# Scores of a cross-attention kernel: from four row tiles of TensorE to eight row-and-column tiles

## The chip, the cores and the metric

The kernel runs on one core of a Trainium2 chip. The metric is the device time of one execution in microseconds, from the runs of the kernel; beside it stands one execution that the hardware profiler recorded, with its trace.

## What is computed

Sixteen batches. `x` is 16 x 100 x 640, the context is 16 x 722 x 384, of which the last 4 tokens (`ca`) are treated apart and 718 are keys and values. There are 8 heads of 80 columns, all in f32. Cut to what matters:

```python
query = x @ Wq                       # 100 x 640
keyt, valt = enc @ Wk, enc @ Wv      # 718 x 640
hs = mha(query, keyt, valt)          # the scores of this change are in here
ca_q1 = einsum('btc,th->bch', ca, Wq_ca)[:, indices]
ca_hs1 = mha(ca_q1, x, x)
ca_hs2 = mha(ca_hs1 @ Wq, ca @ Wk_ca, ca @ Wv_ca)
out = (hs + ca_hs2) @ Wout + b_out + x

def mha(q, k, v):                    # per head, d = 80
    scores = q @ k.T * d ** -0.5     # 100 x 718
    return softmax(scores) @ v
```

## The kernel before, in words

One long program without loops on the device; Python writes out all instructions, batch after batch, and from the first batch on each engine executes them in the order in which they are written (`manual_schedule`). TensorE, VectorE (DVE), ScalarE (ACT), GpSimd (POOL) and SyncE (SP) wait for each other by semaphores.

The 718 keys of a batch lie in three thirds `u` of 240 (they overlap by a key), each in two halves `j` of `KN` = 120 keys: six blocks `KC`. The transposed keys are in `kT`, [128, 5, 3, 240]: the head dimension of 80 is cut into 64 + 16, and spread so that chunks `c` = 0 to 3 hold, in each of the four groups of 32 partitions (row groups, `r`), 32 rows of one head; chunk 4 holds the remaining 16 rows of two heads in each row group. The queries lie in the same way in `qp` (chunks 0 to 3, 100 columns per product) and `qz` (chunk 4, where two heads' queries stand side by side with zeros, 200 columns).

`scores(b, g, tiles)` is called three times in a batch, for `g` = 0, 1, 2, each for two of the six blocks (`a` = 0, 1). For every block and chunk it issues one product in each row group (L612): 32 rows, 120 key columns as weights, 100 or 200 query columns streamed, into the PSUM bank `s_ps[r]` of that row group. That is 2 x 5 x 4 = 40 products for each `g`, 120 in a batch, 1920 in all. A product in f32 shows in the trace as two weight loads (PEld) and two matmuls (PE). The banks of `g` = 0 and 2 come as two pairs from the pool `ps2`, the four of `g` = 1 from `psk` and `ps1`. ScalarE copies them to the tile `st` (L629 for the pairs, L623 for the single banks); VectorE folds `st` into a running maximum `most` (L1246, L1234).

The order of a batch on TensorE around the scores: the products of probabilities and values of the batch before (`a_ps`, L1419: pairs of column tiles, 64 and 36 query rows), the scores (L612), then `z_ps` (L788, `softmax2`: four column tiles of 32, 32, 32 and 4 rows, 33 columns streamed), then `y_ps` (L736), and then the long stretch in which this batch's values (`v_ps...`, L432) and the next batch's keys (`k_ps...`, L463, and `kT_ps`, L557) are made, with the output projection (`o_ps`, L1013) or the next queries (`q_ps`, L533) in some batches. Meanwhile VectorE and ScalarE turn the maximum, subtract it (L1222) and take the exponentials (L1230), and GpSimd makes sums for the keys and values (L498) and the second attention (L761, L768, L855, L862).

## Time and profile before

| | us |
|---|---|
| median of 3 runs | 931.06 |
| lowest and highest of them | 929.72, 931.26 |
| profiled execution: span from the first to the last instruction | 929.5 |
| TensorE matmuls busy | 922.4 (99%) |
| TensorE weight loads busy | 787.6 (85%) |
| VectorE busy | 693.2 (75%) |
| GpSimd busy | 678.2 (73%) |
| ScalarE busy | 433.9 (47%) |

For the profiled execution no other time than its span is given; it lies within the runs' lowest 0.3 us. PE are matmuls and PEld weight loads, which go beside each other. Matmuls are pipelined and their recorded ends are modelled, so times from start to start say more than durations. "issue" as the releaser of idle time means that the engine waited for nothing that the profile shows. Queues of the kind "instruction" bring the engines' own code from memory.

### The profile page before, as it was taken

The numbers are of one execution on the slowest core, as the hardware profiler recorded it, in microseconds if no ns is written. First come the engines' busy times: TensorE is split into PE (matmuls) and PEld (weight loads), VectorE is DVE, ScalarE is ACT, GpSimd is POOL, SyncE is SP. The second block draws the span as 40 slices with busy tenths as digits, with TensorE's granted clock in tenths as the row PEclk, the third lists the DMA queues.
The fourth block names the chain that finished last, engine by engine and source line by source line (L and its number), as shares of the span: only waits on it lengthen the run. The fifth ranks groups of instructions, "written<-read, shape, count | busy, mean of one in ns | idle before, by whom it ended". The sixth has DMA issues, their size and how long they took to land.

```text
span 929.5 us, 25894 instructions
## 1 busy us (share of the span) xinstructions
PE 922.4 (99%) x11130; PEld 787.6 (85%) x11130; DVE 693.2 (75%) x1085; ACT 433.9 (47%) x836; POOL 678.2 (73%) x646
## 2 busy tenths in 40 slices
PE   9999999999999999999999999999999999999998
PEld 6998989797897979888798788988879888797966
DVE  3859895989739896685967869579873888838884
ACT  2234543736337363652726436264641737427341
POOL 5757998788938877496884968758895578956724
PEclk9999999999999999999999999999999999999999
DMA  8722022040300304031030400205030050310201
GB/s 262 264 85 77 25 66 76 7 149 2 117 17 23 105 13 120 2 103 53 28 105 3 120 36 30 75 2 154 2 103 30 2 154 2 102 45 2 82 19 41
DMA packets 49673, 62.82 MB, mean 68 GB/s; under 512 B 14072, under 2 KB 38200, under 8 KB 49560
## 3 DMA queue, kind: packets, MB, share of 16 engines
q1 hardware_dynamic: 45512, 51.49, 18.3%
q0 software_dynamic: 3024, 8.53, 3.0%
q8 instruction: 87, 1.43, 0.6%
q10 hardware_dynamic: 1024, 1.15, 0.4%
q14 instruction: 26, 0.21, 0.1%
HBM read 55.59 MB, written 5.57 MB: 66 GB/s over the span
## 4 chain that ended last, share of the span: by engine, by line
PE 97%; DVE 2%; DMA 0%; issue 0%; ACT 0%; POOL 0%; ACTq 0%; DVEq 0%
PE s_ps L612 12%; PE a_ps L1419 12%; PE v_psA L432 11%; PE v_psB L432 9%; PE kT_ps L557 8%; PE k_psA L463 7%; PE q_ps L533 7%; PE k_psB L463 6%; PE o_ps L1013 5%; PE v_psC L432 3%; PE k_psC L463 3%; PE v_psD L432 2%; PE v_psE L432 2%; PE y_ps L736 2%; PE v_ps L373 1%; PE k_psE L463 1%
## 5 line engine op out<-in xcount | busy, mean ns | idle before, releaser
L761 POOL TENSOR_TENSOR e<-ca,g 100x800 f32<-100x800 f32 x64 | 99.4, 1564 | 126.8 <-DVE most L1234 99.7
L498 POOL TENSOR_TENSOR enc<-enc 128x240 f32<-128x240 f32 x135 | 106.7, 800 | 19.7 <-DMA enc<-in_enct 12.7
L1222 DVE TENSOR_TENSOR st<-st,over 120x1600 f32<-120x1600 f32 x48 | 117.0, 2439 | 0.0
L1419 PEld LDWEIGHTS a_ps<-vs,st 120*36 120x36 f32 (+3 forms) x3072 | 109.3, 125 | 5.9 <-issue 5.8
L1419 PE MATMUL a_ps<-vs,st 120*36 120x81 f32 (+3 forms) x3072 | 112.2, 233 | 0.9 <-issue 0.9
L432 PE MATMUL v_psA<-wv_sb,enc 128*120 128x320 f32 x352 | 109.8, 434 | 0.0
L862 POOL TENSOR_TENSOR hs<-hs,hs 100x640 f32<-100x640 f32 x48 | 100.5, 2095 | 3.8
L612 PE MATMUL s_ps<-qp,kT 32*120 32x100 f32 x3072 | 97.5, 263 | 0.0
L855 POOL TENSOR_TENSOR hs<-vb,p 100x640 f32<-100x640 f32 x64 | 89.6, 1411 | 9.5 <-issue 4.7
L612 PEld LDWEIGHTS s_ps<-qp,kT 32*120 32x120 f32 x3072 | 94.7, 179 | 1.7 <-issue 0.2
L629 ACT COPY st<-s_ps 120x800 f32<-120x800 f32 x64 | 49.7, 828 | 98.1 <-PE s_ps L612 98.1
L768 POOL TENSOR_TENSOR e<-e,e 100x800 f32<-100x800 f32 x48 | 92.0, 1917 | 3.8
L432 PE MATMUL v_psB<-wv_sb,enc 128*120 128x320 f32 x296 | 91.8, 433 | 0.0
L1230 ACT ACTIVATE st<-st 120x1600 f32<-120x1600 f32 x48 | 73.9, 1539 | 32.3 <-DVE st L1222 32.1
L463 PE MATMUL k_psA<-enc,wk_sb 128*128 128x240 f32 x360 | 87.7, 366 | 0.0
L1234 DVE TENSOR_TENSOR most<-most,st 120x800 f32<-120x800 f32 x64 | 69.0, 1078 | 21.9 <-ACT st L623 20.8
L463 PEld LDWEIGHTS k_psA<-enc,wk_sb 128*128 128x128 f32 x360 | 68.3, 190 | 16.7
L432 PEld LDWEIGHTS v_psA<-wv_sb,enc 128*120 128x120 f32 x352 | 63.2, 183 | 22.6 <-DVE vs L403 0.5
L463 PE MATMUL k_psB<-enc,wk_sb 128*128 128x240 f32 x300 | 73.1, 366 | 0.1
L432 PEld LDWEIGHTS v_psB<-wv_sb,enc 128*120 128x120 f32 x296 | 54.1, 183 | 21.9 <-DVE vs L403 0.4
L928 ACT COPY hsT<-turned_hs 32x160 f32<-32x160 f32 (+7 forms) x244 | 67.7, 278 | 3.0
L533 PE MATMUL q_ps<-xT,wq_sb 128*128 128x200 f32 x400 | 69.1, 333 | 0.0
(168 smaller groups left out, 1802.9 us busy)
## 6 DMA issues: line engine op xcount, KB each, us to landing
vb<-va_d POOLq DMA_DIRECT2D x32, 250.0 KB, 3.5
vb<-va_d SPq DMA_DIRECT2D x32, 250.0 KB
enc<-in_enct SPq DMA_DIRECT2D x30, 240.0 KB
enc<-in_enct SPq DMA_DIRECT2D x15, 360.0 KB
xT<-in_xt SPq DMA_DIRECT2D x8, 500.0 KB
rest<-in_enct SPq DMA_DIRECT2D x31, 120.0 KB
xn<-in_x SPq DMA_DIRECT2D x11, 320.0 KB
out<-xn SPq DMA_DIRECT2D x11, 320.0 KB
```

The source lines that it names most:

```text
L432: nc.tensor.matmul(at[0][j][:KN, : H // 2], a_form(self.enc, f)[:, j * KN : (j + 1) * KN], wv_there.get(f, wv_sb[:, W_AT[f]]), start=first ...
L463: nc.tensor.matmul(at[:, i * KT : (i + 1) * KT], wk_sb[:, W_AT[f], i], a_form(self.enc, f), start=(first and i == 0), stop=last, skip_grou ...
L498: nc.gpsimd.tensor_tensor(out, left, right, op)
L533: nc.tensor.matmul(q_ps[:, : 2 * S].rearrange("p (j s) -> p j s", j=2), wq_sb[:, c, n * P : (n + 1) * P], xT[:, :, c, :], start=(c == 0), ...
L557: nc.tensor.matmul(bank[:, i * KT : (i + 1) * KT], weights[c], a_raw(enc, u, c), start=(i == 0 and c == 0), stop=(c == CC - 1), skip_group ...
L612: nc.tensor.matmul(s_ps[r][:n, 256 * a + lo : 256 * a + hi], kT[rows, c, u, j * KN : (j + 1) * KN], rhs, start=(a == 0 and c == 0), stop=( ...
L761: first = nc.gpsimd.tensor_tensor(to, self.ca[:, t, :].unsqueeze(1).to_broadcast([S, NH, S]), g[:, :, t].unsqueeze(2).to_broadcast([S, NH, ...
L768: nc.gpsimd.tensor_tensor(e, e, to, ALU.add)
L855: first = nc.gpsimd.tensor_tensor(to, self.vb[t][:S].rearrange("p (h d) -> p h d", h=NH), p2[:, :, t].unsqueeze(2).to_broadcast([S, NH, D] ...
L862: nc.gpsimd.tensor_tensor(sums, sums, to, ALU.add)
L1222: return nc.vector.tensor_tensor(st[i], st[i], top.over[:KN].unsqueeze(1).to_broadcast([KN, 2, ROWS]), ALU.subtract,)
L1419: nc.tensor.matmul(a_v[lo:hi, h % 4], st[i // 2][: KEYS[i], i % 2, h * S + lo : h * S + hi], block(i, h // 4)[: KEYS[i], h % 4], start=(i ...
```

## The change

In `scores`, each product of a row group is written as two: keys 0 to 63 of the block go to the PSUM partitions 0 to 63, keys 64 to 119 to the partitions 64 to 119 of the same bank. With the four row groups, TensorE is then used as eight tiles of 32 rows by 64 columns. The streamed queries, the banks, the copies and the order of everything else remain. 1920 products become 3840, so the scores' weight loads and matmuls go from 3840 each to 7680 each. All lines below L612 in the file move down by one.

```diff
                         rhs, lo, hi = qz[rows, 0, b % 2], 0, 2 * S
-                    nc.tensor.matmul(
-                        s_ps[r][:n, 256 * a + lo : 256 * a + hi],
-                        kT[rows, c, u, j * KN : (j + 1) * KN],
-                        rhs,
-                        start=(a == 0 and c == 0),
-                        stop=(c == HC - 1),
-                        skip_group_check=True,
-                    )
+                    for k0, k1 in ((0, 64), (64, n)):
+                        nc.tensor.matmul(
+                            s_ps[r][k0:k1, 256 * a + lo : 256 * a + hi],
+                            kT[rows, c, u, j * KN + k0 : j * KN + k1],
+                            rhs,
+                            start=(a == 0 and c == 0),
+                            stop=(c == HC - 1),
+                            skip_group_check=True,
+                        )
```

## The prediction

> **What bounds the kernel now.** I read the page first, then the groups of instructions with their shapes kept apart, then one batch in the timeline, then the stages around the change, and last the few places where TensorE stood still without a wait. The page:

> ```profile
> span 929.5 us, 25894 instructions
> PE 922.4 (99%) x11130; PEld 787.6 (85%) x11130; DVE 693.2 (75%) x1085; ACT 433.9 (47%) x836; POOL 678.2 (73%) x646
> ...
> q8 instruction: 87, 1.43, 0.6%
> ...
> PE 97%; DVE 2%; DMA 0%; issue 0%; ACT 0%; POOL 0%; ACTq 0%; DVEq 0%
> PE s_ps L612 12%; PE a_ps L1419 12%; PE v_psA L432 11%; PE v_psB L432 9%; PE kT_ps L557 8%; PE k_psA L463 7%; PE q_ps L533 7%; PE k_psB L463 6%; PE o_ps L1013 5%; PE v_psC L432 3%; PE k_psC L463 3%; PE v_psD L432 2%; PE v_psE L432 2%; PE y_ps L736 2%; PE v_ps L373 1%; PE k_psE L463 1%
> ```

> TensorE is the bound from end to end, and the scores are 12% of that chain. So each microsecond that the scores win or lose shows in the span, as long as TensorE stays the last. One line matters later: 11130 loads and 11130 matmuls go through TensorE, and queue q8 brings 87 packets of instructions. 22260 / 87 is 256 instructions to a packet of 16 KB: this is TensorE's own code, fetched while it runs.

> The scores' line (durations minimum / median / maximum), and the loads of other widths:

> ```profile
> L612 PEld LDWEIGHTS s_ps<-qp,kT x3072: 174/180/180, 60.0 to 885.6; 32*120 32x120 f32 x192
> L612 PE MATMUL s_ps<-qp,kT x3072: 244/263/342, 60.0 to 885.7; 32*120 32x100 f32 x192
> L612 PE MATMUL s_ps<-qz,kT x768: 327/338/413, 60.9 to 886.0; 32*120 32x200 f32 x192
> ```
> ```profile
> L1419 PEld LDWEIGHTS a_ps<-vs,st 120*64 120x64 f32 x1024 | 84.5, 136 | 5.9 <-issue 5.8
> ...
> L463 PEld LDWEIGHTS k_psA<-enc,wk_sb 128*128 128x128 f32 x360 | 68.3, 190 | 16.7
> ...
> L788 PEld LDWEIGHTS z_ps<-y_sb,e 100*4 100x4 f32 x256 | 9.1, 84 | 0.0
> ```

> Per batch there are 120 products in the scores, and (3072 + 768) / 16 = 240 matmuls and 240 loads: each f32 product is two loads and two matmuls. A hundred more columns stream in 327 - 244 = 83 ns. Loads of 128 and of 4 columns differ by 106 ns, 0.855 ns a column: a load of 120 columns occupies its row group for 103 ns, one of 64 for 55. So today a 100-column product is bound by its load (103), not by its stream (83). One batch in the timeline:

> ```profile
> 431.77 1.10 PE L612 MATMUL s_ps<-qp,kT 32*120 32x100 f32 x32
> 432.69 0.54 PE L612 MATMUL s_ps<-qz,kT 32*120 32x200 f32 x8
> 433.05 1.00 PE L612 MATMUL s_ps<-qp,kT 32*120 32x100 f32 x32
> ...
> 438.58 0.54 PE L612 MATMUL s_ps<-qz,kT 32*120 32x200 f32 x8
> 439.05 0.75 PE L788 MATMUL z_ps<-y_sb,e 100*32 100x33 f32 x64
> ```

> From 432.69 to 438.58 lie five blocks of keys, 1.178 us each. Per row group that is 8 steps of 103 ns and 2 of 167 (200 columns, stream-bound): 1.158, so the reading holds.

> The same batch by stages: attention times values (a_ps), scores, z_ps, and all that follows up to the next a_ps (columns: window, its length, then busy time and count of TensorE's matmuls, its loads, VectorE, ScalarE and GpSimd, the granted clock, DMA share, GB/s).

> ```profile
> 424.85:431.77 6.92, 6.92 (x193) 6.82 (x193) 4.53 (x7) 0.87 (x1) 6.61 (x9) 1.00 0.27 99
> 431.77:439.05 7.28, 7.28 (x243) 7.04 (x241) 4.00 (x6) 3.23 (x6) 3.17 (x4) 1.00 0.01 2
> 439.05:439.72 0.67, 0.67 (x68) 0.63 (x64) 0.64 (x2) 0.52 (x1) 0.00 (x0) 1.00 0.11 24
> 439.72:481.22 41.50, 41.50 (x208) 35.12 (x199) 35.68 (x55) 23.05 (x49) 32.55 (x29) 1.00 0.24 74
> ```

> **The change, first part: what the array gains.** Each product of 120 key columns becomes two, of 64 and 56, in the two column tiles of its row group. The longer load now takes 55 ns and hides behind the 83 ns stream. That column tiles run side by side shows in a_ps, which already pairs 64 with 36 columns: 193 matmuls in 6.92 us are 72 ns a pair, against 81 x 0.83 = 67 for one stream; two after another would be 134. The extra is 5 ns. So a step becomes 83 + 5 = 88 and a 200-column step 167 + 5 = 172: 8 x 88 + 2 x 172 = 1.048 us instead of 1.178. Six blocks in 16 batches: 96 x 0.130 = 12.5 us less, if the instructions are there in time.

> Nothing else in the order moves; ScalarE's copies (L629, L623) and VectorE's maxima (L1246, L1234) stay behind the scores. Were the scores faster, the cover would be this: copies of group 0 must free their banks before group 2 starts.

> ```profile
> 434.49 1.55 ACT L629 COPY st<-s_ps 120x800 f32<-120x800 f32 x2 [5.22 <-PE s_ps L612]
> 436.83 1.68 ACT L623 COPY st<-s_ps 120x400 f32<-120x400 f32 x4 [0.79 <-PE s_ps L612]
> 439.20 1.55 ACT L629 COPY st<-s_ps 120x800 f32<-120x800 f32 x2 [0.69 <-PE s_ps L612]
> ```

> A group would last 2.10 us and the longest set of copies 1.68, so ScalarE keeps up; at worst some 0.1 us a batch returns, 2 us in all.

> **Second part: what the change adds.** The scores' instructions double: per batch 480 more loads and matmuls, 7680 in all, 30 more packets of code. Does code arrive fast enough? Now it does, barely: 480 instructions in 7.28 us are 3.9 us for 256. Three places show what happens when it does not. TensorE stops with nothing to wait for, in the middle of a_ps and in the middle of z_ps:

> ```profile
> 760.82 2.22 PE L1419 MATMUL a_ps<-vs,st 120*36 120x81 f32 x58
> 763.91 0.79 PE L1419 MATMUL a_ps<-vs,st 120*64 120x81 f32 x17 [0.87 <-issue]
> ```
> ```profile
> 381.10 0.57 PEld L788 LDWEIGHTS z_ps<-y_sb,e 100*32 100x32 f32 x57 [0.24 <-issue]
> 381.94 0.15 PEld L788 LDWEIGHTS z_ps<-y_sb,e 100*32 100x32 f32 x7 [0.26 <-issue]
> ```

> Between the two restarts TensorE ran this many instructions:

> ```profile
> 381.93:763.90 381.97, 381.11 (x4442) 325.33 (x4442) 291.62 (x460) 190.12 (x374) 286.31 (x265) 1.00 0.21 61
> ```

> 8884, and its semaphore instructions, which are not counted there; 35 packets would be 8960. The stops lie at the edge of a packet. And the code packets stand right before them. The DMA view, in the windows 379.0 to 380.6, then 761.2 to 762.5, then 765.0 to 766.0 (764.0 to 765.0 holds none):

> ```profile
> q8 instruction: 1, 0.02, 5.3%
> ```
> ```profile
> q8 instruction: 1, 0.02, 5.6%
> ```
> ```profile
> q8 instruction: 1, 0.02, 5.8%
> ```

> [...]

> **The sum.** Scores and z_ps (another 128 instructions) come to 1088 a batch, 4.25 packets. About one is in hand when the scores start: half of the one entered, on average, and the next one in half of the batches or nearly there. That one runs at its own pace, 1.68 us; the other 3.25 take 3.6 each, 11.7. Together 13.4 us against 7.28 + 0.67 = 7.95 now: 5.45 more a batch, 87 us in 16. What follows draws 208 matmuls and 199 loads in 41.5 us, 26 us for 256, so it loses nothing and gives nothing back; the other engines have more time than now. The profiled span of 929.5 becomes 1017; the median of the runs, 931.06, lies 1.5 above it and becomes 1018.

> Bounds: with 1.09 + 0.93 + 1.34 = 3.36 for a packet it is +74, with 1.16 + 1.36 + 1.54 = 4.06 it is +111; with half a packet more or less in hand 15 us less or more. As both ends hardly meet, together 995 to 1050. Below nothing only if the fetch hides, which is a rival.

> **Rivals.** *The fetch hides* (faster). If more than one packet is held ahead or a packet comes in under 1.93 us (3.25 times that plus 1.68 is today's 7.95), the array's gain is left: 931 - 12.5, 918.5, up to 920.5 with the copies' 2 us. For it: steps and loads fit the trace closely. Against it: the stops. 11%.

> *Two packets under way at once* (slower, less). If the next one is asked for when the old one is used up rather than when the new one is entered, a packet comes about every (3.6 + 1.68) / 2 = 2.65 us: 10.3 a batch, +38, 969. Against it: the old code had run out by 763.04 (760.82 + 2.22), and the next packet began at 765.0, 2 us after that, but 1.1 after the new one was entered. 8%.

> *The clock falls too.* TensorE would be idle for more than half of each 3.6 us in the scores. Nothing in the trace shows that; over the stretch quoted above, which holds the stop of 1 us, the clock is 1.00. If it halved and the next 3.6 us ran at half speed, that is 1.8 us a batch, 29 more: 1047. 5%.

> *The eight tiles don't overlap*: two column tiles of a row group stream one after the other. A step of 2 x 83 makes a block 2.0 us instead of 1.178, +79, 1010. a_ps speaks against it; by the total alone it couldn't be told from my forecast, by gaps in TensorE it could. 4%.

> **How the numbers follow.** Forecast as summed 72%, at 1018. The range goes from 960 to 1050: it holds the forecast with its bounds, the half-hidden fetch, the clock and the tiles, and leaves out the gain. About 0.2% (2 us) can be told from no change. Faster 0.11; the same 0.01, as only a packet time right at 1.93 us gives it; slower 0.88.

> **What would show it.** If right: about 117 packets on q8; TensorE standing still for 80 to 90 us in the scores and z_ps with "issue" as the releaser; from first score to z_ps 11 to 14 us a batch; in it bursts of 256 instructions some 3.6 us apart, a packet before each; loads of 64 columns at 136 ns, so the array itself quicker. A mean clock near 1.00. Wrong: a stage of 6.3 us with no idle time (the fetch hides), bursts 2.6 us apart (two under way), or a stage without gaps that is longer (the tiles).

## The result, and the profile after

The changed kernel takes 1028.45 us (median of 4 runs, 1025.24 to 1035.74) against 930.57 before (4 runs): 1.106 times as long, interval 1.102 to 1.110. The profiled execution took 1026.92; its span is 95.7 us longer than before. From its page (span, engines, the queue of code, the chain of waits):

```profile
span 1025.2 us, 33574 instructions
PE 943.9 (92%) x14970; PEld 795.2 (78%) x14970; DVE 689.3 (67%) x1085; ACT 434.7 (42%) x836; POOL 673.2 (66%) x646
...
q8 instruction: 117, 1.92, 0.7%
...
PE 91%; issue 7%; DMA 0%; DVE 0%; POOL 0%; ACTq 0%
```

The 117 packets of code are the number worked out ahead. TensorE is still what the chain runs through, but it is busy for 92% of the span instead of 99%, and 7% of the chain is "issue": time in which it waited for nothing that the profile shows. Where, the view of waits tells (TensorE's matmuls, us in total, times, longest):

```profile
PE s_ps L613 <- issue: 58.2, 44, 2.1
PE z_ps L789 <- issue: 14.5, 9, 3.3
PE y_ps L737 <- issue: 2.0, 1, 2.0
```

75 us of stops, in the scores, in z_ps, and once just behind. One batch by windows: a_ps, then scores with z_ps, then what follows.

```profile
343.34:350.26 6.92, 6.92 (x194) 6.83 (x193) 6.48 (x14) 1.69 (x3) 4.67 (x10) 1.00 0.44 117
350.26:363.18 12.92, 8.90 (x546) 7.79 (x544) 5.10 (x7) 3.91 (x7) 7.52 (x10) 1.00 0.02 6
363.18:404.60 41.42, 41.42 (x208) 35.12 (x198) 35.01 (x54) 22.23 (x45) 31.98 (x29) 1.00 0.27 74
```

The stages on both sides take what they took (6.92 and 41.5 before); the middle one takes 12.92 instead of 7.95, and TensorE is busy in 8.90 of that. Over all 16 batches, from the first score to y_ps, the sum is 219.4 against 127.8: a mean of 13.71 a batch against 7.99, +91.6 of the span's +95.7.

The same batch in the timeline of weight loads (start, length, tile, count; in brackets the idle time before):

```profile
350.25 0.83 PEld L613 LDWEIGHTS s_ps<-qp,kT 32*64 32x64 f32 x62
...
351.23 1.03 PEld L613 LDWEIGHTS s_ps<-qp,kT 32*56 32x56 f32 x61
...
354.10 0.62 PEld L613 LDWEIGHTS s_ps<-qp,kT 32*64 32x64 f32 x42 [1.20 <-issue]
...
357.55 0.16 PEld L613 LDWEIGHTS s_ps<-qz,kT 32*64 32x64 f32 x6 [1.63 <-issue]
...
361.55 0.30 PEld L613 LDWEIGHTS s_ps<-qp,kT 32*64 32x64 f32 x22 [1.96 <-issue]
```

While code is in hand, the loads of the first block of 120 keys take 351.23 - 350.25 = 0.98 us. That is no measure of the array, since the loads of a first block run ahead of their matmuls (in the kernel before they take 1.11 us there, the matmuls 1.28). The matmuls of the same two blocks:

```profile
350.26 0.99 PE L613 MATMUL s_ps<-qp,kT 32*64 32x100 f32 x60
...
351.40 1.02 PE L613 MATMUL s_ps<-qp,kT 32*56 32x100 f32 x59
...
352.54 0.57 PE L613 MATMUL s_ps<-qp,kT 32*64 32x100 f32 x20
```

Each block takes 1.14 us, against 1.28 for the first and 1.18 for every other one before. So the array does run faster, but after the first block only a little: over the batches, second blocks without a stop take about 1.16 us, where 1.048 was forecast. Behind them come bursts of 128 loads and 128 matmuls, 256 instructions, that begin 3.45 and 4.00 us apart. Behind the restart at 354.10 the window 354.1 to 355.1 holds no packet of code, and the next one, 355.1 to 356.1, holds this (view of the DMAs; the share is of 16 engines, so 0.88 us):

```profile
q8 instruction: 1, 0.02, 5.5%
```

So it is under way 1.0 us after the burst began, has arrived some 0.9 us after that, and is used 1.5 us later, at 357.55: the order and the three parts of the forecast. The same order stands throughout: all 53 stops of over 0.6 us in the loads, from the scores to y_ps, end 1.2 to 1.6 us after a packet of code has arrived. In 51 of the 53 places the next packet begins 1.0 to 1.7 us after the restart.

### The profile page after: what moved, and what is told of

Read it like the earlier page. It is cut to its first block, busy times and chain, and to the rows that moved or that the text cites. A ratio compares the mean times of both kernels' runs of the same rounds, so it can differ in the third digit from the quotient of the medians.

```text
span 1025.2 us, 33574 instructions
## 1 busy us (share of the span) xinstructions
PE 943.9 (92%) x14970; PEld 795.2 (78%) x14970; DVE 689.3 (67%) x1085; ACT 434.7 (42%) x836; POOL 673.2 (66%) x646
## 3 DMA queue, kind: packets, MB, share of 16 engines
q8 instruction: 117, 1.92, 0.7%
q10 hardware_dynamic: 1024, 1.15, 0.3%
## 4 chain that ended last, share of the span: by engine, by line
PE 91%; issue 7%; DMA 0%; DVE 0%; POOL 0%; ACTq 0%
PE s_ps L613 13%; PE a_ps L1420 11%; PE v_psA L432 10%; PE v_psB L432 8%; PE k_psA L463 7%; PE kT_ps L557 7%; PE q_ps L533 7%; PE k_psB L463 6%; PE o_ps L1014 5%; PE v_psC L432 3%; PE k_psC L463 2%; PE v_ps L373 2%; PE y_ps L737 2%; PE v_psE L432 2%; PE v_psD L432 2%
## 5 line engine op out<-in xcount | busy, mean ns | idle before, releaser
L613 PE MATMUL s_ps<-qp,kT 32*64 32x100 f32 (+1 forms) x6144 | 120.8, 256 | 48.9 <-issue 48.7
L613 PEld LDWEIGHTS s_ps<-qp,kT 32*64 32x64 f32 (+1 forms) x6144 | 105.4, 128 | 60.3 <-issue 56.9
L498 POOL TENSOR_TENSOR enc<-enc 128x240 f32<-128x240 f32 x135 | 101.6, 762 | 19.7 <-DMA enc<-in_enct 12.6
L1223 DVE TENSOR_TENSOR st<-st,over 120x1600 f32<-120x1600 f32 x48 | 114.4, 2385 | 0.0
L432 PE MATMUL v_psA<-wv_sb,enc 128*120 128x320 f32 x352 | 111.1, 438 | 0.0
L863 POOL TENSOR_TENSOR hs<-hs,hs 100x640 f32<-100x640 f32 x48 | 106.4, 2217 | 3.8
L1235 DVE TENSOR_TENSOR most<-most,st 120x800 f32<-120x800 f32 x64 | 65.0, 1016 | 59.7 <-ACT st L624 58.6
L856 POOL TENSOR_TENSOR hs<-vb,p 100x640 f32<-100x640 f32 x64 | 87.1, 1372 | 9.9 <-issue 5.2
L432 PE MATMUL v_psB<-wv_sb,enc 128*120 128x320 f32 x296 | 91.9, 433 | 0.0
L463 PE MATMUL k_psA<-enc,wk_sb 128*128 128x240 f32 x360 | 88.3, 368 | 0.0
L463 PEld LDWEIGHTS k_psA<-enc,wk_sb 128*128 128x128 f32 x360 | 68.9, 192 | 16.8
L432 PEld LDWEIGHTS v_psA<-wv_sb,enc 128*120 128x120 f32 x352 | 63.7, 185 | 22.9 <-issue 1.1
L613 PE MATMUL s_ps<-qz,kT 32*56 32x200 f32 (+1 forms) x1536 | 70.1, 346 | 9.5 <-issue 9.5
L463 PE MATMUL k_psB<-enc,wk_sb 128*128 128x240 f32 x300 | 73.0, 366 | 0.0
L432 PEld LDWEIGHTS v_psB<-wv_sb,enc 128*120 128x120 f32 x296 | 54.3, 184 | 22.2 <-issue 0.4
L533 PE MATMUL q_ps<-xT,wq_sb 128*128 128x200 f32 x400 | 69.1, 333 | 0.0
```

The source lines that it names most:

```text
L432: nc.tensor.matmul(at[0][j][:KN, : H // 2], a_form(self.enc, f)[:, j * KN : (j + 1) * KN], wv_there.get(f, wv_sb[:, W_AT[f]]), start=first ...
L463: nc.tensor.matmul(at[:, i * KT : (i + 1) * KT], wk_sb[:, W_AT[f], i], a_form(self.enc, f), start=(first and i == 0), stop=last, skip_grou ...
L498: nc.gpsimd.tensor_tensor(out, left, right, op)
L533: nc.tensor.matmul(q_ps[:, : 2 * S].rearrange("p (j s) -> p j s", j=2), wq_sb[:, c, n * P : (n + 1) * P], xT[:, :, c, :], start=(c == 0), ...
L613: nc.tensor.matmul(s_ps[r][k0:k1, 256 * a + lo : 256 * a + hi], kT[rows, c, u, j * KN + k0 : j * KN + k1], rhs, start=(a == 0 and c == 0), ...
L856: first = nc.gpsimd.tensor_tensor(to, self.vb[t][:S].rearrange("p (h d) -> p h d", h=NH), p2[:, :, t].unsqueeze(2).to_broadcast([S, NH, D] ...
```

## The experiments

**Two of the four row groups.** The products of row groups 2 and 3 are left out, so the scores issue as many instructions as before the change, in the changed tiles.

```diff
-                for r in range(RG):
+                for r in range(RG // 2):
...
-                    s_ps[r][:n].rearrange(...)
+                    s_ps[r % 2][:n].rearrange(...)
...
-                    pairs[i][:n].rearrange(...)
+                    pairs[0][:n].rearrange(...)
```

> Column tiles kept, code back to the old amount: only the row groups 0 and 1 get their products, each in two column tiles, and the copies read those two banks twice; half of the scores is left out. Per batch 480 loads and matmuls in the scores, as in the kernel before, now at the pace of the column tiles. Code theory (256 instructions cost 3.6 us, whatever the tiles): the stage asks for 256 in about 3.3 us, so hardly a stop, and 12 to 14 us less than before, about 918. Rival (row and column tiles together are slow in themselves, or stream one after the other): a block of keys takes up to 2.0 us instead of 1.18, up to 79 us more than before.

Measured: 920.99 against 930.92, ratio 0.9885 [0.9868, 0.9902]: 9.9 us less, where 12 to 14 were expected. The 16 stages sum to 115.0, 12.8 less than before. A typical one, by windows:

```profile
485.48:492.46 6.98, 6.98 (x307) 6.41 (x304) 3.85 (x6) 3.71 (x7) 0.00 (x0) 1.00 0.02 5
```

No idle time in it, and 6.98 instead of 7.95; a block takes 1.02 us from matmul to matmul. So two column tiles of one row group overlap, and four tiles are no loss. That is not yet eight: with all four row groups a block without a stop takes about 1.16 us. Some 3 of the 12.8 us came back outside the stages. Half of that is one wait of the keys' products for VectorE's `kT` (1.5 us in the view of waits), which the kernel before did not have; the rest I did not trace. In the stage, z_ps's loads now wait for ScalarE's copies of group 1 (4.1 us in 14 places). The prediction had named the copies as the cover, but those of group 0, ahead of group 2.

**The price of a packet.** The kernel before, with 1024 short products at its end that read nothing but a constant.

```diff
+    extra = psum1("extra")
+    for k in range(1024):
+        lo = 32 * (k % 4)
+        nc.tensor.matmul(extra[lo : lo + 32, :33], ident[:S, lo : lo + 32],
+                         ident[:S, :33], start=True, stop=True)
```

> The disputed cost by itself: the kernel before with 1024 products of 32 columns in four column tiles behind its end (100 rows, 33 columns streamed, operands that lie ready, nobody reads them): 4096 loads and matmuls, 16 packets of code. Code theory: about one packet in hand, 15 times 3.6 us: 50 to 58 us more, in bursts 3.4 to 3.9 us apart. If two packets could be under way at once: 15 times 2.0 to 2.6, 30 to 40 us. Rival (code is there in time): 2048 matmuls at the 8.6 to 10.5 ns of z_ps, 18 to 22 us.

Measured: 984.1 us, 1.0566 [1.055, 1.0582]. The added part in the timeline of matmuls:

```profile
927.09 2.42 PE L1453 MATMUL extra<-ident 100*32 100x33 f32 x262
932.18 1.99 PE L1453 MATMUL extra<-ident 100*32 100x33 f32 x128 [2.67 <-issue]
935.65 1.99 PE L1453 MATMUL extra<-ident 100*32 100x33 f32 x128 [1.48 <-issue]
939.67 1.99 PE L1453 MATMUL extra<-ident 100*32 100x33 f32 x128 [2.03 <-issue]
...
980.32 1.92 PE L1453 MATMUL extra<-ident 100*32 100x33 f32 x122 [1.76 <-issue]
```

Thirteen intervals of 3.47 to 4.02 us, (980.32 - 932.18) / 13 = 3.70 for 256 instructions; these products have no operand to wait for and nothing else runs. That settles the price, and two rivals with it: the fetch isn't hidden, and two packets under way at once would have given about (3.6 + 1.99) / 2 = 2.8. The first line shows something else: behind the slower products at the old end, 262 matmuls with their loads, a little over two packets, ran without a stop. So how much is in hand when a dense stretch begins depends on what stands before it. The clock by windows was halved in this stretch:

```profile
932.18:980.32 48.14, 25.87 (x1665) 24.03 (x1664) 0.00 (x0) 0.00 (x0) 0.00 (x0) 0.50 0.02 4
```

The price is the same in the changed kernel, where the mean clock is 0.992: of its restarts after a stop of over 0.6 us in the loads, 36 follow the one before by 3.31 to 4.20 us, with a mean of 3.67. It isn't TensorE's own speed that sets it.

**Twice the code without the tiles, first try.** The kernel before, and beside each product a tiny one of 4 keys and one query column, into spare columns of the bank.

```diff
+                    nc.tensor.matmul(
+                        s_ps[r][:4, 256 * a + 2 * S : 256 * a + 2 * S + 1],
+                        kT[rows, c, u, j * KN : j * KN + 4],
+                        rhs[:, :1], start=False, stop=(c == HC - 1), ...)
```

> The kernel before, four row tiles, no column tiles; behind each product of the scores a tiny one is added in the same row group (4 weight columns, 1 streamed column, into columns of the bank that nobody reads). The amount of code is that of the changed kernel: 960 loads and matmuls a batch. Code theory: 80 to 105 us more than before, about 1010 to 1035, with stops of 1 to 2 us once in 256 instructions. [...]

Measured: 2397.95 us, 2.574 [2.570, 2.578]. No theory of mine had this. The timeline of matmuls:

```profile
339.50 0.45 PE L612 MATMUL s_ps<-qp,kT 32*120 32x100 f32 x2
339.88 0.19 PE L620 MATMUL s_ps<-qp,kT 32*4 32x1 f32 x2
339.99 0.45 PE L612 MATMUL s_ps<-qp,kT 32*120 32x100 f32 x2
340.37 0.19 PE L620 MATMUL s_ps<-qp,kT 32*4 32x1 f32 x2
```

Products of the two widths take turns, 0.49 us a pair, and row groups no longer overlap. So tiles of 120 and of 4 columns did not run beside each other, and the run says nothing on code. The 0.49 is at a clock of 1.00; over whole stages the granted clock was about 0.52 (0.673 over the whole execution), a stage lasted 98 us, and a pair took about 0.81. The prediction had not weighed tiles of two widths.

**Second try**, the same with 65 keys instead of 4: if it was the width that made the products take turns, the wider ones might not.

```diff
-                        s_ps[r][:4, ...], kT[rows, c, u, j * KN : j * KN + 4],
+                        s_ps[r][:65, ...], kT[rows, c, u, j * KN : j * KN + 65],
```

> [...] Four row tiles, no column tiles, 960 loads and matmuls a batch as in the changed kernel. Own pace: two loads of 61 ns more a step, a block of keys 1.79 us instead of 1.18: 55 to 60 us more than before if the code is there in time, without stops (256 instructions in 2.9 us). Code theory (256 instructions cost 3.6 us): 95 to 110 us more, with stops of 0.5 to 1 us at every packet's edge.

Measured: 1037.81 against 931.11, 1.1147 [1.108, 1.121]. The total lies where the theory of code put it, but the view of waits (loads) and a batch by windows don't show its way there:

```profile
PEld s_ps L612 <- issue: 6.5, 13, 0.9
PEld s_ps L620 <- issue: 5.1, 14, 0.9
...
477.51:490.87 13.36, 13.06 (x546) 12.78 (x544) 5.19 (x7) 4.48 (x8) 2.88 (x3) 1.00 0.02 4
```

TensorE stops little and is busy for 13.06 of 13.36 us. These products are slower in themselves than I had worked out: from load to load, a block takes 1.92 to 1.94 us in most places, and 1.94 already as the first of a batch, where code is in hand; 1.79 was expected. Six such blocks and z_ps are some 12.3 of the mean stage's 14.05 us. What lengthens the other blocks, 1.7 us a stage, the run doesn't tell. So the total met the expectation by luck, and it is no evidence for the cause. Beside the first try, where the 20 pairs of a block took 20 x 0.49 = 9.8 us even at full clock, it shows that the width of the small products made the alternation slow there, and not their presence.

**One group of the three.** The changed kernel with the eight tiles in group 0 alone, then in group 2 alone.

```diff
-                    for k0, k1 in ((0, 64), (64, n)):
+                    for k0, k1 in ((0, 64), (64, n)) if g == 0 else ((0, n),):
```

> Eight tiles in the first of the three calls of scores in a batch alone: a third of the added code (160 instructions a batch). Code theory: a threshold, since a part of the added code comes out of what is in hand: 11 to 21 us more than before, less than a third of the whole loss of 98. A cost per added product or per tile: a third of it, 33 us more. Array alone: 4 us less.

> Eight tiles in the third of the three calls of scores in a batch alone: the same added code as e4, at the stage's end, where what was in hand has been used. Code theory: 18 to 24 us more than before, a little more than e4's 18 and less than a third of the whole loss. A cost per added product: 33 us. A cost that depends on the tiles alone: the same as e4.

Measured: group 0 949.17, 1.0193 [1.0176, 1.021]; group 2 961.76, 1.0322 [1.0285, 1.0359]. The stops, for the one and the other:

```profile
PE s_ps L613 <- issue: 7.3, 13, 1.0
```
```profile
PE z_ps L789 <- issue: 11.7, 9, 1.9
PE s_ps L613 <- issue: 4.9, 6, 1.1
```

The same added code costs 18 us at the head of the stage, as expected, and 31 at its end, where the dense z_ps follows; there the expectation ended at 24, a miss. Part of the 31 goes with the granted clock: the profiled run, at 0.998, has a span 25 us longer than before, and the three others are at 0.991 to 0.995. Third of change, third of cost would be 33 for both. The first run rules that out; the second alone wouldn't.

**One block of the six.**

```diff
+                    ... if g == 0 and a == 0 else ((0, n),):
```

> Eight tiles in the first of the six blocks of keys of a batch alone: 80 more instructions a batch, a sixth of the added code. Code theory: the array gains 2 us and what is in hand mostly covers the rest: between 2 us less and 3 us more than before. A cost per added product: 16 us more. It is also the version that could beat both kernels, if any split does.

Measured: 939.35, 1.0085 [1.007, 1.01], +8.2: a miss. The stage sums to 134.9, +7.1. A batch in the timeline of matmuls:

```profile
434.35 0.99 PE L613 MATMUL s_ps<-qp,kT 32*64 32x100 f32 x60
...
435.73 1.10 PE L613 MATMUL s_ps<-qp,kT 32*120 32x100 f32 x32
...
437.00 1.00 PE L613 MATMUL s_ps<-qp,kT 32*120 32x100 f32 x32
```

No stop in it. The split block lasts 435.73 - 434.35 = 1.38 us, though a first block takes 1.13 in the changed kernel, where another split block follows; the next whole one lasts 1.27, as the first did before. What stands between is the change from 64 to 120 columns: together 2.65 against 1.28 + 1.18 before, 0.19 more where a split first block wins 0.15 (1.13 against 1.28), so about 0.3 us for the change of width. In 13 of the 16 batches the split block takes the same 1.38, which speaks against code as the reason. Over 16 batches the 0.19 is 3 of the 7 us; the rest are stops in some batches. The two experiments with one group pay one such change a batch as well, some 5 us each, which their expectations did not hold.

**Work in the stops.** The changed kernel with eight wide products of a constant in the middle of group 2, into spare columns: if TensorE waits for code, work that needs little code should be hidden.

```diff
+            if g == 2 and a == 1:
+                for _ in range(8):
+                    nc.tensor.matmul(s_ps[0][:, 2 * S : 256], ident,
+                                     ident[:, : 256 - 2 * S], start=False, stop=True, ...)
```

> The changed kernel with work added in the scores: in the middle of the third call 8 products of 128 rows, 128 weight columns and 56 streamed columns, into columns that nobody reads: 16 loads of some 110 ns and two changes of the tiles, about 2.1 us a batch, 34 us in all, but only 32 instructions (an eighth of a packet). Code theory: TensorE waits for code there anyway, so the work hides: 0 to 14 us more than the changed kernel, 1028 to 1042. If TensorE is slow for any other reason: 34 us more, 1062.

Measured: 1053.21, 24.8 above the changed kernel: a miss. The four runs lie in two pairs by their granted clock: 1045.75 and 1046.12 at 0.982 and 0.979, 1060.3 and 1061.45 at 0.961 and 0.963. The profiled one is the first of them, 18.8 above the profiled run of the changed kernel. From its groups and waits:

```profile
L606 PE MATMUL s_ps<-ident 128*128 128x56 f32 x256 | 36.7, 303 | 2.0 <-issue 2.0
...
PE s_ps L623 <- issue: 51.0, 38, 2.0
PE s_ps L606 <- issue: 2.0, 2, 1.2
...
PE z_ps L799 <- issue: 0.5, 1, 0.5
```

36.7 us of work were added, and the stops on the matmuls of scores, the added products, z_ps and y_ps fell from 58.2 + 14.5 + 2.0 = 74.7 to 51.0 + 2.0 + 0.5 = 53.5: some 21 us of the work went into stops. The expectation held two changes of the tiles, but not a lower clock (0.982 instead of 0.992 in the profiled runs). The stages tell the two apart. Ten of the 16 hold no stretch at half clock and last 14.1 us on average; the thirteen such stages of the changed kernel last 13.5. So at full clock the added work, 36.7 / 16 = 2.3 us a stage, costs about 0.6 a stage, 9 us in all: it hides for the most part, as the theory of code wants. The six other stages last 16.5 us. Most of the rest of the 18.8 thus goes with the half clock; why it came oftener here, the run doesn't show.

**Less work, the same code.** Two of the five chunks are left out (chunks 1 and 3): 24 products a block instead of 40, in the eight tiles. By the forecast's steps the array needs 4.1 us a batch for the scores (in the trace, blocks without a stop take 0.7 to 0.8 us, some 4.6 in six); the code needs more.

```diff
-            for c in range(HC):
+            for c in (0, 2, 4):
```

> The changed kernel without the chunks 1 and 3 of the scores (that part of the head dimension is left out): the array's work in the scores falls to 6 x 0.68 = 4.1 us a batch, against 6.2 with all chunks and 7.1 in the kernel before, and the code to 576 instructions, a fifth more than the 480 of the kernel before. Code theory: with z_ps 704 instructions, 2.75 packets, one of them in hand: 1.8 + 1.75 x 3.6 = 8.1 us from scores to the end of z_ps, as long as before with far more work: 925 to 940. Rival (TensorE's own pace decides): 4.1 + 0.6 us, 52 us less than before: 879.

Measured: 941.56 against 931.53, 1.0116 [1.009, 1.0141]. A batch by windows, and the waits:

```profile
436.16:444.32 8.16, 5.96 (x355) 5.32 (x353) 5.18 (x7) 4.70 (x8) 2.97 (x3) 1.00 0.02 4
...
PE s_ps L613 <- issue: 22.3, 21, 1.9
PE z_ps L789 <- issue: 7.9, 7, 1.7
```

The total lies just above the 925 to 940 that were expected. The mean stage is 8.11, as worked out from packets (8.1), with two thirds of the columns streamed (2 x 100 + 200 a block and row group instead of 4 x 100 + 200), and it is longer than the 7.99 of the kernel before. This is the sharpest case against every theory in which the array is slow: the array is given less to do, and the time goes by the instructions. Of the profiled span's +9.5 us only 2.0 lie in the stages. Of the 7.5 outside, up to 3.1 go with two half-clock stretches behind stages and 1.4 with one wait of the keys' products for `kT`; the rest was not traced.

## Why the prediction was right

*The array's gain* was mis-sized. With two row groups, so four tiles, a block took 1.02 us and the stages lost 12.8 us where 12.5 were worked out. With all eight tiles a block without a stop took about 1.16 us after the first, instead of 1.18 before and 1.048 in the forecast. Together with the first block (1.13 instead of 1.28) that is at most some 0.15 + 5 x 0.02 = 0.25 us a batch, 4 us in all and not 12.5. The 5 ns in the step of 88 were read from a_ps, which has two column tiles and no row groups; why eight tiles take longer, no run shows. It hardly touched the total, because only about one packet a batch runs at the array's own pace. But had the code been there in time, the kernel would have gained about 4 us, and the first rival's 918.5 would have been some 927.

*The code.* 117 packets; one packet ahead, asked for when the one before is entered; bursts of 256 instructions with a packet in front of each: all three as described, in the changed kernel and, alone, in the added products once their first two packets were used up.

*The sum.* A stage of 13.4 was forecast, 13.71 measured. The term that was mis-sized is the packet: 3.6 forecast, 3.70 measured. 3.25 x 3.70 + 1.68 = 13.7, which is the measured mean, so "about one packet in hand" held on average; it is 5 of the 10 us between forecast and median. That the sum meets the mean so closely is luck: at 1.16 us a block the packet in hand takes 1.86 us and not 1.68, and single stages last from 12.45 to 15.25. The stops were 75 us where 80 to 90 were named: a little under, while the added time (91.6 in the stages) was a little over: matmuls count as busy until their modelled ends (8.90 us in the batch shown, whose clock is 1.00), so part of each stop hides behind them. By the weight loads the stops are 67.0 + 20.9 + 2.1 = 90 us in the same three places.

*The clock* is the other part. I had set it as a rival that either comes or doesn't; in fact it came in some places and added to the forecast. Two windows of the changed kernel, in two batches (the granted clock is the third column from the end):

```profile
118.50:122.00 3.50, 3.50 (x128) 2.85 (x125) 1.39 (x3) 1.55 (x2) 2.66 (x3) 0.55 0.02 5
...
797.80:804.80 7.00, 6.40 (x234) 5.45 (x216) 2.61 (x4) 3.23 (x6) 0.00 (x0) 0.52 0.02 5
```

The mean clock of 0.992 is worth at most 8 us, not the 29 of the rival, since most stops left the clock alone. The spread of the runs goes with it: 1025.24 at 0.993, 1035.74 at 0.982. The +4 us outside the stages are mostly its doing: of 17.1 us at half clock 8.8 lie behind the stages, where TensorE is busy throughout and half a clock costs time. Half of 8.8 is 4.4, and the work behind the first, second and ninth stage, which holds 7.7 of the 8.8, took 1.1, 0.6 and 1.7 us longer than before.

*The rivals.* "The fetch hides": excluded by the added products and by the run with less work. "Two packets under way": excluded by 3.70. "The tiles don't overlap": excluded for four tiles by the run with two row groups, and for eight by the blocks of about 1.16 us, where one after the other would have been 2.0.

*Open.* Whether code can be made to arrive sooner, and whether eight tiles would pay if the scores were spread among the slower products of the long stage behind (208 matmuls in 41.4 us, far less code than it could get), wasn't tried. By the blocks above there would be some 4 us to win, less what a change of width costs. Of the kernels that compute the whole, none beat the kernel before.

## What to carry to other kernels

Count instructions for each microsecond of a stage, not only the array's work: here 256 of TensorE's cost 3.70 us, 14.5 ns each, once a dense stretch had used up what was in hand (about one packet in the changed kernel, a little over two at the start of the added products), and the trace shows it as "issue" stops with a code packet before each restart. Smaller tiles multiply instructions: with 960 instead of 480 in the scores of a batch, the stage went from 7.99 to 13.71 us, and with 480 in the changed tiles it lost 12.8 / 16 = 0.8 us. Measure their gain with all tiles at work: four tiles brought a block from 1.18 to 1.02 us here, eight only to about 1.16. Count the changes of tile width within a stage too: one from 64 to 120 columns took about 0.3 us here.

## What the hardware showed that I had not expected

Products of 120 and of 4 columns took turns, 0.49 us a pair at full clock, while with 65 columns instead of 4 a block of 20 pairs took 1.92 to 1.94 us. A change from 64 to 120 columns took about 0.3 us. Eight tiles in four row groups were slower for each block than four tiles in two (about 1.16 against 1.02 us), though each row group had the same to do. The granted clock halved in or just behind some starved stages (0.55 and 0.52 in the windows above), where no stop of the matmuls was longer than 3.3 us, and through the whole of a long starved stretch (0.50 over 48 us), while the price of a packet stayed as it was (3.70 us in that stretch, 3.67 in the changed kernel).
